# Two-layer metaformer: where the first sample's spectral rows, the filters and the inverse matrices lie between two stages

## The chip, the cores and the metric

The kernel runs on one core of a Trainium2 chip. The core has five engines with queues of their own: TensorE (PE, with PEld for its weight loads), VectorE (DVE), ScalarE (ACT), GpSimd (POOL) and SyncE (SP). SP issues most transfers here; ACT and POOL can issue transfers too. The metric is device microseconds from the first to the last instruction and what lies around them, as the median of several runs.

## What is computed

The input is 16 images of 128 channels by 32 x 32 pixels. The reference, cut to its steps:

```python
# layer 0
x = x + linear_attention(_ln_c(x))          # group norm, q/k softmax, context, projection
t = _to_tokens(x)
t = t + _L0_ffn_ref(_ln_t(t), ...)          # spectral filters (16 filters, FFT convolution) and 3 taps
x = _from_tokens(t, x)
# layer 1
x = x + _L1_conv_ref(_ln_c(x), ...)         # two 3x3 convolutions with batch norm, relu
t = _to_tokens(x)
t = t + _L1_ffn_ref(_ln_t(t), ...)          # 64 experts, each takes its 8 best tokens of a sample
x = _from_tokens(t, x)
```

In the spectral part, `U_plus` and `U_minus` are convolutions of every channel with 16 filters, mixed by `M_phi_plus` and `M_phi_minus` (128 x 128 matrices for each filter). The kernel does this in the frequency domain: at each frequency the spectrum of the samples is multiplied by one 128 x 128 matrix made from the filters.

## The kernel before

There are four stages, one after the other on PE, with overlap at the seams.

**Attention and spectra.** Sixteen samples run through a software pipeline. Each leaves its tokens in DRAM (`xd`) and its spectrum in DRAM (`vd`). The mixed filter matrices are gathered in the tile `mst`, 16 KB in each partition (L216, L685, L687).

**Frequencies.** Sixteen chunks `c` of frequencies. For each, `generate` (L805) makes the matrices from `mst` and `ph`, and `collect` (L816, L818) copies them into a tile `g` of 64 KB in each partition; there are two places for `g`, one for even and one for odd chunks. `multiply` (L829) multiplies the spectra of all samples with them. Chunk c+1 is generated while chunk c is multiplied, so in the last chunk, c = 15, there is only `multiply`. Its results are copied by ACT (L894), combined on DVE (L858, L859) into `ys`, finished (L843 to L846, on POOL, in the last chunk on DVE) and written by SP to the DRAM tensor `yd` in two transfers of 512 KB for each chunk (L850).

**Convolutions and gates.** For each sample b: `load(b)` (L1004) brings its tokens `xt[b]` (512 KB, L1008) and its spectral rows `y` (1 MB in two parts, L1011: 896 KB of rows of chunks 0 to 13, 128 KB of rows of chunks 14 and 15). Two places for `y` alternate between even and odd samples. Then come the small butterflies on POOL and DVE (L1024 to L1054), the `inverse` transform on PE (L1108, with the matrices `wi`, 1 MB, loaded at L956), `add` (L1115), a layer norm, two convolutions in a fast form (L988), the second norm, gates and pooling. The order of this work on every engine and on SP is written out by `planned` from a table with due ranks and is then fixed: an engine works its list in that order even if a later item is ready. In that list DVE has the first butterflies of sample 2 (`odd_sd`, `odd_turn`: L1037 to L1043) ahead of `ab_image` of sample 0 (L1174). POOL's `pair` (L1178) follows `ab_image`, and PE's `conv a` follows `pair`.

Before the list starts, `keep(ps, "cv", 26)` puts 26 matmuls without use on PE (L164, each shown as two rows), which follow the last `multiply`. For sample 0 POOL issues the tokens and the first part of `y`; SP issues everything else. On SP the order is `load(0)`, `load(1)`, then the convolution weights `cw` (two transfers of 1152 KB, L1477), four small biases (L1480, L1482), then `load(2)` and so on.

**Experts.** 32 weight halves of 1 MB go through a ring of 14 places, among them those of `y`, `wi` and `yo`; at the end the results are gated, added and written.

Places in SBUF: tiles of a later stage lie where those of an earlier one lay, and a transfer into such a place waits for the earlier tile's last reader. Adding up the tile sizes, `wi` before lies inside `mst`, whose last reader is the last `generate`.

Of the kernel before, what the change touches and what calls it, by code (L numbers as in the profile page):

```python
# [14 lines left out]
P = 128  # L15
# [15 lines left out]
NQ = 8  # L31
# [38 lines left out]
def metaformer_kernel(ctx: ExitStack, tc: tile.TileContext, io: dict, out: bass.AP):  # L70
# [2 lines left out]
    outs = out.rearrange("b c h w -> b c (h w)")  # L73

    const = ctx.enter_context(tc.tile_pool(name="const", bufs=1))


    ident = const.tile([P, P], F32, name="ident")
# [97 lines left out]
    with ExitStack() as l0:  # L176
# [36 lines left out]
            nc.vector.tensor_tensor(seg[:, i : i + 1], seg[:, i - 1 : i], hard[:, i : i + 1], ALU.add)  # L213
        coef = lconst.tile([P, NF], F32, name="coef")
        nc.vector.tensor_scalar(coef, wmix, sig, None, ALU.mult)
        mst = lconst.tile([P, EPR, C], F32, name="mst")  # L216
        ph = lconst.tile([P, NCH, CW], F32, name="ph")


        with ExitStack() as a0:  # L220
# [427 lines left out]
            def filters():  # L648

                wfm = setup.tile([P, NQ // 2, 2 * P], F32, name="wfm", tag="mi")  # L650
                nc.vector.tensor_scalar(wfm, wf[:, 1::2, :], -1.0, None, ALU.mult)

                def values(q, dst):
                    for sgn in range(2):
                        w = wfm[:, q // 2, :] if sgn and q % 2 else wf[:, q, :]
                        nc.tensor.matmul(
                            dst, phi[:, q, sgn, :], w, start=(sgn == 0), stop=(sgn == 1)
                        )

                yield  # L660
                xf = spectrum_tile()
                for parity in range(2):
                    pe = class_values(parity, values)
                    t = class_copy(pe, 1)
                    ts = class_copy(pe, ROT) if parity else t
                    ab = class_sums(parity, pe, t)
                    class_differences(parity, ab, pe, ts)
                    yield
                    for part in range(2):
                        butterflies(ab, xf, parity, part)  # L670
                    if parity:
                        butterflies(ab, xf, 1, butterflies(ab, xf, 1, 2))
                    yield
                half = CW // 2
                e, o = (xf[:, :, i].rearrange("p c r m j -> p c (r m j)") for i in range(2))
                nc.vector.tensor_tensor(ph[:, :, :half], e, o, ALU.add)
                nc.vector.tensor_tensor(ph[:, :, half:], e, o, ALU.subtract)
                for m in range(EPR // MB):
                    es = slice(m * MB, (m + 1) * MB)
                    for i in range(NF):  # L680
                        mi = setup.tile([P, MB, C], F32, name="mi", tag="mi")
                        nc.sync.dma_start(mi, io["M_phi"][i, :, es, :])
                        yield
                        if i == 0:
                            nc.vector.tensor_scalar(mst[:, es, :], mi, coef[:, 0:1], None, ALU.mult)  # L685
                        else:
                            nc.vector.scalar_tensor_tensor(  # L687
                                mst[:, es, :], mi, coef[:, i : i + 1], mst[:, es, :], ALU.mult, ALU.add
                            )

            def prepare():
# [84 lines left out]
        with ExitStack() as g0:  # L776
# [22 lines left out]
            def generate(c, q):  # L799

                pg = [psg.tile([P, 4, CW], F32, name="pg", tag="p") for r in range(RG)]
                for i in range(4):
                    for r in range(RG):
                        rs = slice(r * KR, (r + 1) * KR)
                        nc.tensor.matmul(  # L805
                            pg[r][:, i], mst[rs, 4 * q + i, :], ph[rs, c, :], start=True, stop=True,
                        )
                return pg

# [28 lines left out]
            def finish(c, ys):  # L838

                eng = nc.gpsimd if c + 1 < NCH else nc.vector  # L840
                e = cpl.tile([P, JL // RG, 2, C], F32, name="ye", tag="ye", bufs=1)
                yv = ys[:, :, 0]
                eng.tensor_tensor(e, yv[:, :, :2], yv[:, :, 2:], ALU.add)  # L843
                eng.tensor_tensor(yv[:, :, 2:], yv[:, :, :2], yv[:, :, 2:], ALU.subtract)
                eng.tensor_tensor(yv[:, :, 0], e[:, :, 0], e[:, :, 1], ALU.add)
                eng.tensor_tensor(yv[:, :, 1], e[:, :, 0], e[:, :, 1], ALU.subtract)  # L846
                for kl in range(JL // RG):
                    last = c + 2 >= NCH
                    j0 = kl * RG + (c - NCH + 2 if last else c) * JL
                    nc.sync.dma_start(  # L850
                        yd[last][j0 : j0 + RG].rearrange("g r b x e -> (g r b) (x e)"),
                        ys[:, kl].rearrange("p x m e -> p (x m e)"),
                    )
# [9 lines left out]
            with tc.manual_schedule(engines=PINNED):  # L863
                begin(0)
                gs[0] = gpl[0].tile([P, CW, C], F32, name="g", tag="g")
                for q in range(NB):
                    collect(0, q, generate(0, q))
                waiting = None
                for c in range(NCH):
                    if c + 1 < NCH:  # L870
                        gs[c + 1] = gpl[(c + 1) % 2].tile([P, CW, C], F32, name="g", tag="g")

                    ys = cpl.tile([P, JL // RG, 2, NM, C], F32, name="ys", tag="ys")
                    for m in range(NM):
                        if c + 1 < NCH:
                            pg = [generate(c + 1, 2 * m + x) for x in range(2)]
                            collect(c + 1, 2 * m, pg[0])
                        if waiting:
                            combine(*waiting)
                        if c + 1 < NCH:  # L880
                            if m == 0:
                                begin(c + 1)
                            collect(c + 1, 2 * m + 1, pg[1])
                        py = psg.tile([P, 2, JL // RG, C], F32, name="py", tag="p")
                        fresh = set()
                        for x in range(2):
                            multiply(c, m, x, py, fresh)
                        if c + 1 < NCH or m == 0:
                            t = cpl.tile([P, 2, JL // RG, C], F32, name="yt", tag="yt", bufs=1)
                        if c + 1 < NCH:  # L890
                            nc.scalar.copy(t, py)
                            waiting = c, m, ys, (t[:, 0], t[:, 1])
                        else:
                            nc.scalar.copy(t[:, m % 2], py[:, 0])  # L894
                            waiting = c, m, ys, (t[:, m % 2], py[:, 1])
                combine(*waiting)


# [11 lines left out]
    with ExitStack() as c1:  # L910
# [14 lines left out]
        FIRST = ("wi", "v", "cw0", "cw1", "p1", "y")  # L925
        halves = {}

        def load_half(h):

# [2 lines left out]
            if g >= E // EG:  # L932
                pr = AWAY[0] + h - 2 * (E // EG)
                if pr in AWAY:
                    tag = RING[(pr - AWAY[0] + 18) % len(RING)]
                    pool = first if tag in FIRST else xpool if tag[:2] == "xp" else work
# [5 lines left out]
            pool = first if tag in FIRST else xpool if tag[:2] == "xp" else work  # L942
            w = pool.tile([P, EG * HID], F32, name=f"we{n}", tag=tag, bufs=RING.count(tag))
            if n == 0:
                nc.sync.dma_start(
# [6 lines left out]
                )  # L952
            halves[h] = w

        wi = first.tile([P, NQ, 2, P], F32, name="wi", tag="wi")
        nc.sync.dma_start(wi, wid)  # L956
        cw = [first.tile([P, 3, NK, C], F32, name=f"cw{n}", tag=f"cw{n}") for n in range(2)]
        gw = cconst.tile([P, E], F32, name="gw")
# [13 lines left out]
        p2 = first.tile([P, 3 * PS - 1 + H * WP], F32, name="p2", tag="p2")  # L972
        nc.gpsimd.memset(p2, 0.0)
        abss = work.tile([P, 4, HT], F32, name="abss", tag="abss", bufs=1)
        yos = work.tile([P, 2, 4, HT], F32, name="yo", tag="yo", bufs=1)

        def of(p, first, step, n=2):

# [20 lines left out]
        def tokens(t):  # L999
            return t.rearrange("p (j c) -> p j c", c=C)  # L1000

        yts, xp = {}, {}

        def load(b):  # L1004
            if b % 2 == 0:
                xp[b // 2] = xpool.tile([P, 2, N], F32, name=f"xp{b // 2}", tag=f"xp{b // 2}")
            xt[b] = xp[b // 2][:, b % 2]
            (nc.sync if b else nc.gpsimd).dma_start(xt[b], xd[b])  # L1008
            yts[b] = first.tile([P, 2, 2 * NM, C], F32, name="y", tag="y", bufs=2)
            for i, js in enumerate((slice(P - 2 * JL), slice(P - 2 * JL, P))):  # L1010
                (nc.gpsimd if b + i == 0 else nc.sync).dma_start(  # L1011
                    yts[b][js].rearrange("p r x e -> p r (x e)"),
                    yd[i][:, :, b].rearrange("j r x e -> j r (x e)"),
                )

# [457 lines left out]
        with tc.manual_schedule(engines=PINNED | {mybir.EngineType.SP}):  # L1473
# [317 lines left out]
```

## Time and profile before

| | |
|---|---|
| median of 4 runs | 1242.4 us (1241.91 to 1244.41) |
| the profiled execution | 1238.34 us, of which its span is 1236.6 us |
| granted TensorE clock, mean | 0.993 |
| PE, DVE, ACT, POOL busy | 94%, 76%, 59%, 49% of the span |
| last `multiply` matmul begins | 652.3 us from the span's start |
| first `inverse` matmul of sample 0 begins | 667.5 us |
| first convolution matmul begins | 688.0 us |

Times inside the execution are microseconds from the span's start. A line of a timeline has the start, the length, the engine, the line of the kernel, the operation, what it writes and reads, and in brackets how long the engine was idle before it and what ended that. "SPq" is SP's queue issuing a transfer. In the chain of waits a row for DMA lasts from a transfer's issue to its landing. In the table of stretches the columns are the busy time of PE, PEld, DVE, ACT and POOL with the number of instructions, the granted clock, the busy share of the 16 DMA engines and what they moved in GB/s.

### The profile page before, as it was taken

The numbers are of one execution on the slowest core, as the hardware profiler recorded it, in microseconds if no ns is written. First come the engines' busy times: TensorE is split into PE (matmuls) and PEld (weight loads), VectorE is DVE, ScalarE is ACT, GpSimd is POOL, SyncE is SP. The second block draws the span as 40 slices with busy tenths as digits, with TensorE's granted clock in tenths as the row PEclk, the third lists the DMA queues.
The fourth block names the chain that finished last, engine by engine and source line by source line (L and its number), as shares of the span: only waits on it lengthen the run. The fifth ranks groups of instructions, "written<-read, shape, count | busy, mean of one in ns | idle before, by whom it ended". The sixth has DMA issues, their size and how long they took to land.

```text
span 1236.6 us, 34361 instructions
## 1 busy us (share of the span) xinstructions
PE 1158.5 (94%) x14398; PEld 952.8 (77%) x14398; DVE 936.6 (76%) x1944; ACT 724.8 (59%) x1420; POOL 603.6 (49%) x800
## 2 busy tenths in 40 slices
PE   6889999999999999999997899999999999998996
PEld 5677777777767889888887788888888888886453
DVE  5888888888766677677674689898988989876235
ACT  4777787777655777777670444565555565554211
POOL 2435454655568688888793433343433333230003
PEclk9999999999999999999998999999999999999998
DMA  7005334253436344443348611223333321406899
GB/s 281 24 31 169 120 114 156 94 171 102 154 120 197 97 137 135 132 130 128 111 135 272 160 52 52 86 76 120 95 120 116 107 86 68 154 34 224 318 403 383
DMA packets 91243, 175.14 MB, mean 142 GB/s; under 512 B 5968, under 2 KB 42064, under 8 KB 90448
## 3 DMA queue, kind: packets, MB, share of 16 engines
q1 hardware_dynamic: 90448, 170.46, 41.2%
q0 software_dynamic: 640, 2.49, 0.6%
q8 instruction: 113, 1.85, 0.6%
q14 instruction: 42, 0.34, 0.1%
HBM read 110.28 MB, written 62.65 MB: 140 GB/s over the span
## 4 chain that ended last, share of the span: by engine, by line
PE 55%; DVE 22%; issue 11%; ACT 5%; DMA 4%; POOL 2%; SPq 0%; POOLq 0%; DVEq 0%; ACTq 0%
PE pg L805 10%; PE pcv L988 10%; PE py L829 10%; PE big L638 6%; DVE bst L135 4%; PE big L171 3%; PE big L152 3%; PE big L570 3%; PE big L450 2%; PE big L533 2%; PE big L432 2%; DVE abss L1231 1%; DVE xp L1253 1%; DVE xp L1115 1%; ACT tt L144 1%
## 5 line engine op out<-in xcount | busy, mean ns | idle before, releaser
L988 PE MATMUL pcv<-v,cw 128*128 128x256 f32 x1152 | 258.2, 380 | 2.2 <-POOL v L1178 2.2
L988 PEld LDWEIGHTS pcv<-v,cw 128*128 128x128 f32 x1152 | 215.0, 190 | 35.0 <-issue 4.9
L818 ACT COPY g<-pg 128x512 f32<-128x512 f32 x316 | 161.1, 606 | 45.2 <-PE pg L805 44.5
L816 DVE COPY g<-pg 128x512 f32<-128x512 f32 x196 | 127.8, 683 | 72.1 <-PE pg L805 72.1
L805 PE MATMUL pg<-ph,mst 32*128 32x128 f32 x4096 | 142.7, 279 | 9.2 <-issue 7.9
L805 PEld LDWEIGHTS pg<-ph,mst 32*128 32x128 f32 x4096 | 127.6, 186 | 25.4 <-issue 15.9
L829 PE MATMUL py<-g,v 128*32 128x128 f32 x4096 | 124.9, 274 | 1.9 <-POOL v L797 1.2
L829 PEld LDWEIGHTS py<-g,v 128*32 128x32 f32 x4096 | 108.1, 110 | 9.8 <-POOL v L797 1.5
L144 ACT ACTIVATE tok<-tok,sts 128x128 f32<-128x128 f32 x256 | 101.9, 480 | 17.0 <-DVE sts L1065 13.6
L135 DVE BATCH_NORM_STATS2 bst<-big 128x6 f32<-128x256 f32 x256 | 91.2, 418 | 20.8 <-PE big L152 11.7
L796 POOL TENSOR_TENSOR v<-xc 128x256 f32<-128x256 f32 x128 | 99.6, 802 | 3.5 <-DMA xc<-vd 3.5
L638 PE MATMUL big<-u,mu 128*128 128x128 f32 (+4 forms) x384 | 86.1, 380 | 0.0
L1178 POOL TENSOR_TENSOR v<-abss 128x256 f32<-128x256 f32 x64 | 49.1, 787 | 68.1 <-DVE abss L1174 56.7
L286 POOL TENSOR_TENSOR xf<-ab 128x256 f32<-128x256 f32 x34 | 24.7, 727 | 110.6 <-DVE ab L253 110.6
L1197 POOL TENSOR_TENSOR yo<-abss 128x256 f32<-128x256 f32 x32 | 23.5, 734 | 108.6 <-DVE abss L1193 108.6
L638 PEld LDWEIGHTS big<-u,mu 128*128 128x128 f32 x384 | 56.8, 191 | 18.0 <-issue 15.3
L570 PE MATMUL big<-wf,ub 128*128 128x256 f32 x256 | 62.0, 385 | 0.2
L144 ACT ACTIVATE tt<-tt,sts 128x128 f32<-128x128 f32 x128 | 51.1, 480 | 14.6 <-DVE sts L1065 14.6
L797 POOL TENSOR_SCALAR v<-v 128x256 f32<-128x256 f32 x64 | 55.4, 866 | 5.6
L475 POOL TENSOR_TENSOR ke<-ke,ks 128x1024 f32<-128x1024 f32 x16 | 30.6, 1912 | 55.1 <-DVE qs L483 43.5
L570 PEld LDWEIGHTS big<-wf,ub 128*128 128x128 f32 x256 | 46.2, 190 | 8.7 <-ACT xn L423 3.0
L144 ACT ACTIVATE ub<-ub,sts 128x128 f32<-128x128 f32 x128 | 50.8, 481 | 0.0
(256 smaller groups left out, 2475.4 us busy)
## 6 DMA issues: line engine op xcount, KB each, us to landing
we<-in_weight SPq DMA_DIRECT2D x32, 1024.0 KB, 9.5
xc<-vd SPq DMA_DIRECT2D x64, 256.0 KB, 3.3
yd<-ys SPq DMA_DIRECT2D x32, 512.0 KB, 3.8
vd<-xf SPq DMA_DIRECT2D x15, 1024.0 KB, 5.1
y<-yd SPq DMA_DIRECT2D x15, 896.0 KB, 6.3
x<-in_x SPq DMA_DIRECT2D x16, 512.0 KB, 5.1
mi<-in_M_phi SPq DMA_DIRECT2D x16, 512.0 KB, 4.8
xd<-x SPq DMA_DIRECT2D x16, 512.0 KB, 6.3
```

Source lines behind the costliest of these rows:

```text
L135: nc.vector.bn_stats(bst[:, j : j + 2, :].rearrange("p j s -> p (j s)"), src[:, j : j + 2, :].rearrange("p j c -> p c j"),)
L144: nc.scalar.activation(dst[:, j, :], src[:, j, :], AF.Identity, bias=nm[:, j : j + 1], scale=r[:, j : j + 1],)
L570: nc.tensor.matmul(dst, self.ub[:, q, :], wf[:, q, :], start=True, stop=True)
L638: nc.tensor.matmul(self.pa[:, a:hi], mu[:, NF - 1 - si, tap, :], self.u[:, a - tap : hi - tap], start=(tap == 0), stop=(tap == KU - 1),)
L796: nc.gpsimd.tensor_tensor(vv[:, x, 1:, bs], e, o, op)
L797: nc.gpsimd.tensor_scalar(v[:, :, 0, bs], v[:, :, 2, bs], -1.0, None, ALU.mult)
L805: nc.tensor.matmul(pg[r][:, i], mst[rs, 4 * q + i, :], ph[rs, c, :], start=True, stop=True,)
L816: nc.vector.tensor_copy(dst, src)
L818: nc.scalar.copy(dst, src)
L829: nc.tensor.matmul(py[rows, x, kl, :], v[:, (x * NM + m) * JL + jl, 1 - ri : 3 - ri, :] .rearrange("p k b -> p (k b)"), g[:, ((x * 2 + ri) ...
L988: nc.tensor.matmul(pc[:, i], wt[:, dy, k, :], v[:, k, dy * WT : dy * WT + HT], start=(dy == 0), stop=(dy == 2),)
L1178: nc.gpsimd.tensor_tensor(v[:, k, WT : WT + HT], self.ab[:, 0], self.ab[:, 1], op)
```

## The change

The filters `mst` become two tiles of 8 KB that share a new pool, and a tag, with `y`; that pool lies ahead of all others and stays through the later stages. `y` of sample 0 therefore lies where the first half of `mst` lay, and `y` of sample 1 where the second half lay. `yo` goes from the pool `work` to `first`, `wi` from `first` to `work`, as the first tile there; by the sizes, it starts 6.5 KB into the 64 KB place of the odd chunks' `g`, which the last chunk uses.

The rows of sample 0 no longer come by `load(0)`. After the last chunk's matmuls have been put in the list, ACT issues two transfers from `yd`: the rows of chunks 0 to 13 and those of chunk 14. The last chunk's rows go from `ys` straight into `y` by four transfers of four partitions by 4 KB, two on SP and two on ACT, ahead of the writes to `yd`, which stay. The tokens of sample 0 come by SP instead of POOL, and for sample 1 `y` is issued ahead of the tokens. `keep` has 13 instead of 26.

```diff
+    ypool = ctx.enter_context(tc.tile_pool(name="ypool", bufs=2, reuse_waits="tile"))
+    yts = {}
+
+    def load_y(b, q, parts):
+
+        if b not in yts:
+            yts[b] = ypool.tile([P, 2, 2 * NM, C], F32, name="y", tag="y", bufs=2)
+        for j0, j1, i, k in parts:
+            q.dma_start(
+                yts[b][j0:j1].rearrange("p r x e -> p r (x e)"),
+                yd[i][k : k + j1 - j0, :, b].rearrange("j r x e -> j r (x e)"),
+            )
...
-        mst = lconst.tile([P, EPR, C], F32, name="mst")
+        mst = [
+            ypool.tile([P, EPR // 2, C], F32, name=f"mst{i}", tag="y", bufs=2) for i in range(2)
+        ]
+
+        def mrow(i, n=1):
+            h, k = divmod(i, EPR // 2)
+            return mst[h][:, k : k + n]
...
-                            pg[r][:, i], mst[rs, 4 * q + i, :], ph[rs, c, :], start=True, stop=True,
+                            pg[r][:, i], mrow(4 * q + i)[rs, 0], ph[rs, c, :], start=True, stop=True,
...
                 eng.tensor_tensor(yv[:, :, 1], e[:, :, 0], e[:, :, 1], ALU.subtract)
+                for kl in range(JL // RG if c + 1 == NCH else 0):
+                    for r in range(2):
+                        j0 = P - JL + kl * RG
+                        (nc.scalar if kl else nc.sync).dma_start(
+                            yts[0][j0 : j0 + RG, r].rearrange("p x e -> p (x e)"),
+                            ys[r * B :: 2 * B, kl].rearrange("p x m e -> p (x m e)"),
+                        )
...
+                load_y(0, nc.scalar, ((0, P - 2 * JL, 0, 0), (P - 2 * JL, P - JL, 1, 0)))
                 combine(*waiting)
...
-        wi = first.tile([P, NQ, 2, P], F32, name="wi", tag="wi")
+        wi = work.tile([P, NQ, 2, P], F32, name="wi", tag="wi", bufs=1)
         nc.sync.dma_start(wi, wid)
...
-        yos = work.tile([P, 2, 4, HT], F32, name="yo", tag="yo", bufs=1)
+        yos = first.tile([P, 2, 4, HT], F32, name="yo", tag="yo")
...
-            (nc.sync if b else nc.gpsimd).dma_start(xt[b], xd[b])
-            yts[b] = first.tile([P, 2, 2 * NM, C], F32, name="y", tag="y", bufs=2)
-            for i, js in enumerate((slice(P - 2 * JL), slice(P - 2 * JL, P))):
-                (nc.gpsimd if b + i == 0 else nc.sync).dma_start(
-                    yts[b][js].rearrange("p r x e -> p r (x e)"),
-                    yd[i][:, :, b].rearrange("j r x e -> j r (x e)"),
-                )
+            if b != 1:
+                nc.sync.dma_start(xt[b], xd[b])
+            if b:
+                load_y(b, nc.sync, ((0, P - 2 * JL, 0, 0), (P - 2 * JL, P, 1, 0)))
+            if b == 1:
+                nc.sync.dma_start(xt[b], xd[b])
...
-            keep(ps, "cv", 26)
+            keep(ps, "cv", 13)
```

The helper `pool_of` gives each tag of the expert ring its pool after the moves; the order of the ring is the same.

More of the change, by code (lines that the diff above doesn't have):

```diff
@@ L684, in filters @@
                         if i == 0:
-                            nc.vector.tensor_scalar(mst[:, es, :], mi, coef[:, 0:1], None, ALU.mult)
+                            nc.vector.tensor_scalar(mrow(m * MB, MB), mi, coef[:, 0:1], None, ALU.mult)
                         else:
                             nc.vector.scalar_tensor_tensor(
-                                mst[:, es, :], mi, coef[:, i : i + 1], mst[:, es, :], ALU.mult, ALU.add
+                                mrow(m * MB, MB), mi, coef[:, i : i + 1], mrow(m * MB, MB), ALU.mult, ALU.add
                             )
@@ L924, in metaformer_kernel, with pool_of @@
         )
-        FIRST = ("wi", "v", "cw0", "cw1", "p1", "y")
+        FIRST = ("yo", "v", "cw0", "cw1", "p1")
         halves = {}
+        def pool_of(tag):
+            return first if tag in FIRST else xpool if tag[:2] == "xp" else ypool if tag == "y" else work
         def load_half(h):
@@ L935, in load_half @@
                     tag = RING[(pr - AWAY[0] + 18) % len(RING)]
-                    pool = first if tag in FIRST else xpool if tag[:2] == "xp" else work
+                    pool = pool_of(tag)
                     x = pool.tile([P, 2, N], F32, name=f"xb{pr}", tag=tag, bufs=RING.count(tag))
@@ L941, in load_half @@
                 return
-            pool = first if tag in FIRST else xpool if tag[:2] == "xp" else work
+            pool = pool_of(tag)
             w = pool.tile([P, EG * HID], F32, name=f"we{n}", tag=tag, bufs=RING.count(tag))
@@ L1000, in tokens @@
             return t.rearrange("p (j c) -> p j c", c=C)
-        yts, xp = {}, {}
+        xp = {}
         def load(b):
```

## The prediction

> **What bounds the kernel now.** The page says PE, at 94% of the span, so a change at the seam of two stages is worth the PE idle time that it takes out there. I therefore read the chain of waits around the seam first: start, length, what.
>
> ```profile
> 645.22 7.41 PE py L829 x256
> ...
> 655.65 0.35 DVE ys L846
> ...
> 656.37 7.60 DMA yd<-ys
> ...
> 664.17 0.63 SPq L1011
> ...
> 677.09 11.29 DMA y<-yd
> ...
> 691.50 0.61 DVE abss L1174
> ...
> 692.18 0.73 POOL v L1178
> ...
> 692.95 5.45 PE pcv L988 x24
> ```
>
> The chain leaves PE with the last multiply at 652.63 and returns for good at 692.95, with conv a of sample 0. Between them are two round trips through DRAM: chunk 15's writes and the last part of sample 0's y (667.3), and then the queue of transfers that brings sample 2's y at 688.38. The timeline shows how the two hold the engines.
>
> ```profile
> 645.49 0.43 SPq L956 DMA_DIRECT2D wi<-wid  x1
> 652.55 11.49 PE L164 MATMUL wm<-ident 128*128 128x256 f32 x52
> 667.50 1.13 PE L1108 MATMUL big<-wi,y 128*128 128x128 f32 x8 [3.46 <-DMA y<-yd]
> 673.95 0.33 SPq L1008 DMA_DIRECT2D xp<-xd  x1
> 688.48 0.42 DVE L1037 TENSOR_TENSOR z<-y 128x256 f32<-128x256 f32 x1 [4.63 <-DMA y<-yd]
> 692.95 5.45 PE L988 MATMUL pcv<-v,cw 128*128 128x256 f32 x24 [2.17 <-POOL v L1178]
> ```
>
> The reader is to see that sample 0's y costs PE a late start (667.5), but that the second wait, sample 2's butterflies in front of `ab_image` in DVE's fixed list, decides when conv a starts. ACT had `image_copy` (L1165) done at 687.96, so `ab_image` could have run then; it ran at 691.50, and PE stood 2.17 us. Last the table of stretches, for the transfers:
>
> ```profile
> 654.00:656.00 2.00, 2.00 (x11) 1.77 (x10) 1.91 (x4) 0.00 (x0) 0.00 (x0) 1.00 0.94 217
> 656.00:658.00 2.00, 2.00 (x11) 1.77 (x10) 0.00 (x0) 0.00 (x0) 0.00 (x0) 1.00 0.97 373
> 658.00:660.00 2.00, 2.00 (x11) 1.74 (x11) 0.00 (x0) 0.00 (x0) 0.00 (x0) 1.00 1.00 404
> 662.00:664.00 2.00, 2.00 (x10) 1.46 (x8) 0.00 (x0) 0.00 (x0) 0.00 (x0) 1.00 0.12 47
> 672.00:674.00 2.00, 2.00 (x12) 2.00 (x11) 0.42 (x2) 0.00 (x0) 0.00 (x0) 0.50 0.89 228
> ```
>
> The DMA engines are full from 651.3 to 690 but for about 3.0 us (662.3 to 665.3), when SP waits for the writes to land.
>
> **The change, part by part.**
>
> *Direct rows.* They take out the write (656.0 to 663.97), SP's issue at 664.17 and its 3.1 us. In place: four transfers of 16 KB, issued at 656.0 to 656.9 when DVE is done. The nearest rows are the small loads `gb` and `tmat` (0.2 and 64 KB), 2.1 to 2.4 us to landing, so 658.2 to 659.3 if nothing is ahead of them in the queues. [...]
>
> *wi.* It goes from 645.49, an empty queue, to the last reader of chunk 15's `g`: not before 652.63. Alone it took 5.7 us, which gives 658.4. But chunk 14's writes (1.05 MB, from 651.3) are ahead of it on SP, and ACT's two loads of y (1.05 MB, issued from 653.1, after its last copy) run beside it: 3.15 MB. At 0.38 MB/us this is through at 659.6, and landed at about 660.4. I take 0.38 from the rows 373, 404 and 399 GB/s of 656 to 662, when loads and writes ran on two queues; in the 217 row the software queue was alone, and the change uses it no more. At 0.26 (the 652 to 654 row) it is 663.4. So inverse 0 starts at 660.4, 7.1 us earlier, with bounds 658.5 and 663.5.
>
> *Dummies.* 52 rows in 11.49 us, 0.221 each; 26 rows end at 658.3. The gap to the inverse is 2.1 us, against 3.46 now, after which the clock stood at 0.50 from 669 to 675 and the last 16 inverse matmuls took 3.79 us instead of the 2.05 of sample 1. [...]
>
> *Sample 0's chain.* DVE has sample 1's butterflies ahead of `stats` of sample 0 (677.88 now). Sample 1's second y part must still wait for chunk 15's writes; behind them and x0 it lands at about 669.8, two DVE pairs take 1.5 us, and `stats` begins at 671.5: 6.4 us earlier. So much is this chain worth if nothing else holds it; a warm clock doesn't change that.
>
> *Moved issues.* x0 goes to SP, behind chunk 15's writes; it lands by 664.5 and `add` needs it at 666.5 at the earliest, so it hides behind the inverse (6 us); without that cover it costs up to 1.4 us. ACT's four issues, 0.6 us each, and its wait for chunk 14's writes (2.6 us for such a write in a free queue, so about 654.5) cost nothing: after its last copy ACT is idle for 26.3 us. If they come late, only the two direct transfers behind them do. SP has two issues more (about 0.4 each) ahead of chunk 15's writes. A ninth transfer waits until that eight places before it has landed: x2 was issued at 673.95 when y1's first part landed (665.47 + 8.5). So chunk 15's second write probably waits for wi, to about 660; the queue is full until then, so nothing is added. POOL loses two issues of 0.7 us, off the path. Splitting `mst` and moving `yo` issue the same instructions into places as free as before; with no cover they would cost 0, bounds -0.5 and +0.5 us.
>
> *The queue up to sample 2's y.* What must pass first: chunk 14's writes, wi, y0, chunk 15's writes (1.05 MB each) and x0 (0.52): 4.72 MB from 651.3. At 0.38 this ends at 663.7. Then comes the list that began before at 667.3 (y0's last part landed) and ended at 688.38, 21.1 us: x1, y1, cw, biases, x2, y2. So y2 lands at 684.8. The first part at the 0.322 that 651.3 to 662.3 averaged before (3.54 MB in 11 us) gives 687.1; at 0.40, 684.2.
>
> *Sum.* From y2's landing to conv a it was 692.95 - 688.38 = 4.57 us. Conv a starts at the later of 690.78 - 6.4 = 684.4 (sample 0's chain without PE's 2.17) and 684.8 + 4.57 = 689.4: 3.6 us earlier. PE is 96% busy from 700 to 772 and 95 to 100% in every stretch of 24 us from there to 1110, and the later loads of y aren't awaited by it, so the 3.6 us pass to the end. The profiled 1238.34 becomes 1234.7; it lies 4.1 below the median shown, so I state 1242.4 - 3.6 = **1238.8 us**, own range 1237.7 to 1241.6 from the two rates and the 0.5 of the moved tiles.
>
> **Rivals.**
>
> *A. Sample 2's y doesn't bind.* If the list of 21.1 us runs as fast as its best rows (433 and 406 GB/s at 674 to 678), its 5.7 MB and the 0.7 that overtook it take 16 us, y2 lands at 679.7, and the chain of sample 0 decides: 6.4 us, 1236.0. For it: two queues run less with y alone. Against: loads of y took 6.1 to 6.4 us for 0.92 MB even in an empty queue.
>
> *B. The seam is DMA-bound and wi's megabyte eats the gain.* From 651.3 to y2's landing 10.1 MB moved in 37.1 us less 3.0 idle: 0.296 MB/us. With wi 11.1 MB at that rate take 37.6 us: y2 at 688.9, time 1242.9, no change. For it: the mean is the safest rate. Against: it contains the software queue's slow rows.
>
> *C. Slower: the same megabyte at the rate of the rows 668 to 674* (295, 244, 228, mean 0.256; y loads fill them, and there are more of these beside wi now). With a rate of 0.27 over the whole, y2 lands at 692.4 and the time is 1246.4. It decides by over 0.2% once the mean falls under 0.281 (11.1 MB by 690.8). Against: it would need to be below what before reached.
>
> **How the numbers follow.** Forecast 0.47, A 0.22, B 0.18, C 0.13. The measurement can tell 0.2%, 2.5 us, from no change: faster is below 1239.9. Of the forecast 0.38 lies there, 0.09 within; with A, faster is 0.60; same, with B, 0.27; slower 0.13. The range goes from 1235.0 (A with a shorter list) to 1243.5 (B with run spread), leaving out most of C.
>
> **What would show it.** Right: the first L1108 near 660.4, wi issued right after the last L829, y2's landing near 685 with DVE's L1037 still ended by DMA, conv a near 689. Wrong: L1037 not waiting (A); y2 at 688 or later though L1108 is early (B, C). If SP has wi behind chunk 15's writes, the inverse starts at 663 and the sum stays. If L1108 stays near 667, the direct rows aren't the last to land and my first step fails.

## The result and the profile after

The kernel became slower by a quarter of a per cent: 1245.56 us as the median of 53 runs (1238.27 to 1253.9), beside 1242.34 us for 77 runs of the kernel before; the ratio is 1.0024 with a 95% interval of 1.0013 to 1.0034, so between 1.6 and 4.2 us, and 3.0 in the middle. The forecast of 1238.8 was on the wrong side of it, and its range too low. The profiled execution took 1242.1 us (span 1240.3).

In the new profile the last `multiply` ends at 648.72 instead of 652.62, though nothing ahead of it runs other instructions. The frequency stage simply varies: over the sixteen profiles of this study it took from 266 to 279 us, with a mean of 274 us for both layouts (five and eleven profiles; with this spread a difference of 2 us between the layouts would not show). So all times of the seam are given below from the end of the last `multiply` in the same profile, written +10 for 10 us behind it. The mark for the whole seam is the first matmul of sample 2's `inverse`, behind conv a: from there to the last sample's `inverse` every kernel takes the same 354.3 to 354.9 us.

The chain of waits of the kernel after, in the same stretch as shown of before (start, length, what):

```profile
641.53 7.23 PE py L848 x256
...
651.77 0.35 DVE ys L865
...
652.13 0.66 SPq L869
...
653.93 6.82 DMA yd<-ys
...
660.83 0.60 SPq L84
...
671.77 11.05 DMA y<-yd
...
685.94 0.61 DVE abss L1203
...
686.62 0.73 POOL v L1207
...
687.39 7.08 PE pcv L1018 x24
```

It is the same chain as before; SP's two issues of direct rows (652.13 to 653.39) now stand in it, ahead of the writes. PE's own wait is still for sample 2's y. That y is in use at +34.2 (682.92 less 648.72), where it was at +35.9. And the end of the chain has a new row: conv a's 24 rows take 7.08 us, where they took 5.45. The timelines of the kernel after, by engine:

```profile
648.65 5.88 PE L176 MATMUL wm<-ident 128*128 128x256 f32 x26
648.81 0.32 SPq L986 DMA_DIRECT2D wi<-wid  x1
658.52 0.76 PE L1137 MATMUL big<-wi,y 128*128 128x128 f32 x2 [4.00 <-DMA y<-ys]
660.50 1.62 PE L1137 MATMUL big<-wi,y 128*128 128x128 f32 x6 [1.21 <-DMA y<-ys]
682.92 0.42 DVE L1066 TENSOR_TENSOR z<-y 128x256 f32<-128x256 f32 x1 [5.21 <-DMA y<-yd]
687.39 7.08 PE L1018 MATMUL pcv<-v,cw 128*128 128x256 f32 x24 [2.75 <-POOL v L1207]
```

Sample 0's rows are complete at +11.8, before at +14.7. The gain is 2.9 us, and it does not reach conv a: PE's gap in front of it grew from 2.17 to 2.75 us. The stretches say why conv a itself became longer (columns as before: busy PE, PEld, DVE, ACT, POOL, then granted clock, DMA share, GB/s):

```profile
656.00:658.00 2.00, 0.00 (x0) 0.00 (x0) 0.00 (x0) 0.00 (x0) 0.00 (x0) 0.65 1.02 363
658.00:660.00 2.00, 0.76 (x2) 0.50 (x2) 0.00 (x0) 0.00 (x0) 0.00 (x0) 0.50 0.98 358
666.00:668.00 2.00, 2.00 (x12) 2.00 (x10) 0.00 (x0) 0.00 (x0) 0.00 (x0) 0.50 0.96 305
686.00:688.00 2.00, 0.61 (x2) 0.52 (x3) 2.00 (x6) 0.09 (x1) 1.91 (x3) 0.83 0.97 221
688.00:690.00 2.00, 2.00 (x6) 1.64 (x5) 1.83 (x8) 0.42 (x2) 0.28 (x2) 0.50 0.40 137
```

After the 13 dummies PE stands from 654.5 to 658.5, the clock falls to 0.50 and is still there in the stretch 670 to 672. It falls a second time between 686 and 688 (a mean of 0.83, then 0.50), at the end of the gap in front of conv a; before, conv a ran at 1.00 (in the stretches from 692 to 700). The DMA engines are full until 688 (a share of 0.90 or more in every stretch of 2 us from 648). Together sample 2's `inverse` starts at +48.64, before at +48.67: the whole change moved nothing in the seam. So the 3 us lie behind the seam, or in the scatter ahead of it.

### The profile page after: what moved, and what is told of

The parts are those of the page before. It is cut to its first block, busy times and chain, and to the rows that moved or that the text cites. A ratio compares the mean times of both kernels' runs of the same rounds, so it can differ in the third digit from the quotient of the medians.

```text
span 1240.3 us, 34315 instructions
## 1 busy us (share of the span) xinstructions
PE 1159.5 (93%) x14372; PEld 953.5 (77%) x14372; DVE 938.4 (76%) x1944; ACT 724.9 (58%) x1420; POOL 601.8 (49%) x798
## 3 DMA queue, kind: packets, MB, share of 16 engines
q8 instruction: 113, 1.85, 0.6%
## 4 chain that ended last, share of the span: by engine, by line
PE 54%; DVE 22%; issue 11%; ACT 6%; DMA 4%; POOL 2%; SPq 1%; POOLq 0%; ACTq 0%; DVEq 0%
PE pg L824 10%; PE pcv L1018 10%; PE py L848 10%; PE big L657 6%; DVE bst L147 4%; PE big L164 3%; PE big L183 3%; PE big L589 2%; PE big L469 2%; PE big L552 2%; PE big L451 2%; DVE abss L1260 1%; DVE xp L1282 1%; DVE xp L1144 1%; ACT ub L568 1%
## 5 line engine op out<-in xcount | busy, mean ns | idle before, releaser
L824 PEld LDWEIGHTS pg<-ph,mst 32*128 32x128 f32 x4096 | 127.6, 186 | 21.9 <-issue 13.6
L156 ACT ACTIVATE tok<-tok,sts 128x128 f32<-128x128 f32 x256 | 101.9, 480 | 17.0 <-DVE sts L1094 13.6
```

Of the source, the lines that this page charges most:

```text
L156: nc.scalar.activation(dst[:, j, :], src[:, j, :], AF.Identity, bias=nm[:, j : j + 1], scale=r[:, j : j + 1],)
L824: nc.tensor.matmul(pg[r][:, i], mrow(4 * q + i)[rs, 0], ph[rs, c, :], start=True, stop=True,)
```

## The experiments

The table has all kernels that were run. "y2 in use" is DVE's first butterfly of sample 2, "gap" PE's idle time in front of conv a, "conv a" its 24 rows (a dash where conv a followed without a gap on conv c, the 12 rows of a convolution ahead of it), "inverse 2" the mark of the seam, "end" the time from the first gate matmul (L1624 in before) to the end. Ratios are to the kernel before, run beside it in the same batch; its medians there were 1244.91 (first four), 1245.37 (next four) and 1243.13 (next four). The last two have one run each.

| kernel | inverse 0 | y2 in use | gap | conv a | inverse 2 | end | ratio [95%] |
|---|---|---|---|---|---|---|---|
| before | +14.9 | +35.9 | 2.17 | 5.45 | +48.67 | 26.0 | |
| after | +9.8 | +34.2 | 2.75 | 7.08 | +48.64 | 27.2 | 1.0024 [1.0013, 1.0034] |
| after, 26 dummies | +11.3 | +35.1 | 4.69 | 7.13 | +49.62 | 26.1 | 1.0011 [0.9989, 1.0033] |
| after, `wi` early | +8.4 | +34.1 | 5.69 | 7.70 | +49.12 | 27.7 | 1.0046 [1.0025, 1.0066] |
| after, `wi` early, 26 | +11.3 | +33.4 | 5.27 | 7.12 | +47.86 | 26.3 | 1.0009 [0.9990, 1.0028] |
| before, 13 dummies | +10.9 | +33.3 | 4.96 | 7.89 | +48.56 | 27.6 | 1.0037 [1.0019, 1.0054] |
| after, 26, filters late | +12.1 | +30.3 | - | - | +44.86 | 26.2 | 0.9947 [0.9929, 0.9966] |
| before, filters late | +13.8 | +29.8 | - | - | +44.88 | 26.0 | 0.9976 [0.9955, 0.9997] |
| after, 26, order | +11.3 | +36.1 | - | - | +48.20 | 26.2 | 0.9986 [0.9969, 1.0004] |
| before, order | +14.8 | +38.7 | - | - | +49.42 | 26.0 | 0.9964 [0.9943, 0.9986] |
| after, 26, filters late, `wi` early | +11.3 | +28.2 | 0.26 | 5.45 | +41.06 | 26.3 | 0.9942 [0.9920, 0.9964] |
| the same with 13 | +7.9 | +29.8 | 1.25 | 5.45 | +42.65 | 27.9 | 0.9963 [0.9942, 0.9985] |
| before, 39 dummies | +16.9 | +33.5 | 1.85 | 5.45 | +46.31 | 26.0 | 0.9997 [0.9977, 1.0016] |
| after, 26, filters late, no direct rows | +22.0 | +36.8 | - | - | +51.85 | 26.4 | 1.0034 [1.0012, 1.0057] |
| after, 13 more at logits | +12.0 | +35.6 | 4.91 | 7.03 | +49.99 | 26.2 | one run |
| after, filters late, `wi` early, 13 more at logits | +7.7 | +28.4 | 0.88 | 5.45 | +41.17 | 26.4 | one run |

The scatter of the frequency stage is in every median, so a ratio alone can't tell two kernels of this table apart by less than about 0.2%; the columns of the seam can. Seam and ratio do not always agree: the two kernels with filters late and no other column far apart (+44.86 and +44.88, 26.2 and 26.0) have ratios 0.29% apart.

### First round: dummies or the queue

The two theories were called CLOCK (the 13 missing dummies let PE's clock fall) and QUEUE (the megabyte of `wi` and the order of transfers set the seam). Four kernels cross them.

Kernel after with 26 dummies:

```diff
-            keep(ps, "cv", 13)
+            keep(ps, "cv", 26)
```

> The changed kernel with 26 dummy matmuls again. Theory CLOCK (the 13 missing dummies let PE's clock fall to half at the seam, 657 to 673 and again from 687): the clock stays at 1.00 until the inverse, conv a of sample 0 runs its 24 rows in about 5.4 us instead of 7.1, the stretch from the last multiply to sample 2's first inverse matmul falls from 48.6 to about 47 us, and the median falls by 2 to 4 us below the changed kernel's, to the kernel before or up to 1.5 us under it. Theory QUEUE (wi's megabyte and the order of transfers set the seam, the clock is a side effect): the stretch stays within 0.5 us of 48.6 and the median stays about 3 us above before.

Measured: 1.0011, interval 0.9989 to 1.0033. Sample 2's `inverse` did not move forward; conv a in the profile is as slow as with 13, behind a longer gap, with a mean clock of 0.84 over 694 to 698 and 0.73 over 698 to 702:

```profile
688.96 2.76 PE L1018 MATMUL pcv<-v,cw 128*128 128x256 f32 x12
696.40 7.13 PE L1018 MATMUL pcv<-v,cw 128*128 128x256 f32 x24 [4.69 <-POOL v L1207]
```

So the dummies keep the clock in front of `inverse` 0 (1.00 from 664 to 680 us, that is +7 to +23, where the kernel after had 0.50 from about +8), and it is lost 30 us later: what sample 0's chain is earlier, PE waits longer for POOL's `pair`, and conv a pays for the wait a second time (7.13 us instead of 5.45 in before).

Kernel after with `wi` back in its early place (13 dummies), and the same with 26:

```diff
-        FIRST = ("yo", "v", "cw0", "cw1", "p1")
+        FIRST = ("wi", "v", "cw0", "cw1", "p1")
-        wi = work.tile([P, NQ, 2, P], F32, name="wi", tag="wi", bufs=1)
+        wi = first.tile([P, NQ, 2, P], F32, name="wi", tag="wi")
-        yos = first.tile([P, 2, 4, HT], F32, name="yo", tag="yo")
+        yos = work.tile([P, 2, 4, HT], F32, name="yo", tag="yo", bufs=1)
```

> The changed kernel with wi and yo back in their pools, so that wi lies under the even chunks' g, which is free before the last chunk's matmuls, and is loaded ahead of chunk 14's writes; 13 dummies as in the change. QUEUE: wi's 1.05 MB (about 2.8 us at 0.38 MB/us) leaves the seam's transfers, the direct rows land about 2.5 us earlier (9.3 us instead of 11.8 after the last multiply), sample 2's y 2.5 to 3 us earlier (31 to 31.6 us after it instead of 34.1), median about 2 to 3 us under the changed kernel. CLOCK: conv a still runs at half speed, the stretch to sample 2's inverse falls by under 1 us, median within 1 us of the changed kernel.

> wi early and 26 dummies. CLOCK and QUEUE each give their part: if both hold the stretch from the last multiply to sample 2's inverse falls to about 44.5 us (1.6 from the clock, 2.5 from the queue) and the median lies 3 to 5 us under the kernel before. If only CLOCK holds it is as with 26 dummies alone; if only QUEUE holds, as with wi early alone. If neither, it stays near 48.6 and the loss lies outside the seam.

Measured 1.0046 and 1.0009. Sample 0's rows came at +8.4 with 13, but sample 2's y was in use at +34.1 and +33.4, where it had been at +34.2 and +35.1 with the late `wi`: a gain of nothing and of 1.7 us, where 2.5 to 3 were expected, and with one and the same queue y2 scatters by 2.6 us (last section). QUEUE failed there.

The kernel before with 13 dummies:

> The kernel before with 13 dummies, nothing else. CLOCK: PE idles for 9 us instead of 3.5 ahead of sample 0's inverse, the clock falls earlier and the median rises by 1 to 4 us, about as much as the change did. QUEUE: PE waits there for transfers in any case, the median stays within 1 us of before.

Measured 1.0037. Of both pairs (13 against 26 with `wi` early; before with 13 against before) the one with 13 is slower by about 4 us in the medians, and by 2.8 to 3.0 us in the profiles from the last `multiply` to the end of the span. That looked like CLOCK, but for two things in the table: the seam accounts for +1.3 and -0.1 us of it, and the end column, 26.0 in the kernel before, is longer by 1.2 to 1.9 in every kernel with only 13, some 550 us behind the dummies.

### Second round: what decides conv a

If y2, which DVE's fixed list has ahead of `ab_image` of sample 0, decides conv a, then either bringing y2 sooner or taking it out of the way must move the seam. Filters late:

```diff
-            for n in range(2):
-                nc.sync.dma_start(cw[n], cwd[n])
+            nc.sync.dma_start(cw[0], cwd[0])
...
                     if b > 1:
                         load(b)
+                    if b == 2:
+                        nc.sync.dma_start(cw[1], cwd[1])
```

(The four bias transfers move with `cw[1]`.) On the kernel after with 26 dummies, and on the kernel before:

> After with 26 dummies; the second half of the filters (1.05 MB) and the four biases are issued behind y2 instead of in front of it, so y2 comes 4 to 5 us earlier than in the run with 26 dummies alone (last multiply to y2 in use +35.1 there). ORDER (sample 2's y, in front of ab_image of sample 0 on VectorE, is what decides): the 4.7 us of PE's gap in front of conv a go, conv a follows conv c at once and keeps the clock (24 rows 5.4 instead of 7.1 us), inverse 2 starts 4 to 4.5 us earlier than +49.6, time about 1241 beside 1245.3 for 26 dummies alone. CLOCK alone (what the seam needs is a warm clock): inverse 2 within 1 us of +49, time 1244 to 1246.

> Before with the same move of filters and biases behind y2. ORDER: y2 ceases to decide, sample 0's own late chain (inverse 0 at +14.9) does; conv a at about +38.1 instead of +40.3, inverse 2 at about +46.5 instead of +48.7, ratio about 0.998. Beside the run on after with 26 dummies the difference, about 2 us, is what the early rows are worth once y2 is out of the way. CLOCK alone: within 0.1% of before.

Measured 0.9947 and 0.9976; conv a follows conv c without a gap in both. The surprise is the seam: +44.86 and +44.88. With y2 out of the way the direct rows should have been worth 2 us, and they are worth nothing. The chain of waits of each tells why; first the kernel after with 26 and late filters:

```profile
656.86 8.40 DMA wi<-wid
665.28 4.75 DMA y<-ys
...
674.27 3.80 PE big L1137 x16
```

and the kernel before with late filters, whose last `multiply` ended at 661.42:

```profile
665.16 6.39 DMA yd<-ys
...
671.75 3.24 DMA y<-yd
...
679.20 3.51 PE big L1108 x16
```

In the first, the last of the direct rows come in at 670.03, that is +13.2 (656.79 subtracted). A DMA row of the chain begins with the issue, so the fourth direct transfer was issued only at 665.28, when `wi` had landed; `wi` waits for the end of the last `multiply` (it is issued 0.07 us behind it) and takes 8.40 us here. The other three were issued by 661.4. In the kernel after, the same wait would be short: it is read from the length of ACT's two issues, which take 2.21 us there and 1.14 us where `wi` is early:

```profile
652.24 2.21 ACTq L869 DMA_DIRECT2D y<-ys  x2
```

The first two `inverse` matmuls, which need two of the other three transfers, ran at 668.92 and the next at 670.16, so by estimate this wait accounts for 1.2 us; the rest is the slower passage beside `wi`, 6.8 and 7.1 us from issue to landing for SP's two direct transfers, which took 4.1 and 4.4 us with early `wi` and late filters (third round). In the second kernel, the round trip through DRAM ends at 674.99, that is +13.6. The edit exchanges one wait for another of the same length.

The order, changed by hand in the fixed list:

```diff
+        late = [(2, n) for n in ("even", "odd_sd", "odd_t", "odd_turn")]
+        order = [o for o in order if o not in late]
+        at = order.index((0, "pair")) + 1
+        order[at:at] = late
```

> After with 26 dummies; in the order that is written out by hand the four steps of sample 2's y (even, odd_sd, odd_t, odd_turn) come behind the pair of sample 0, so y2 lands as before but nobody in front of conv a waits for it. ORDER: gap in front of conv a gone, conv a directly behind conv c, inverse 2 at about +45 instead of +49.6, time about 1241; inverse 2's own wait for sample 2's y must then not take it back. CLOCK alone: inverse 2 within 1 us of +49.6.

> Before with the same four steps moved behind the pair of sample 0. ORDER: conv a about 2.2 us earlier, inverse 2 at about +46.5 instead of +48.7, ratio about 0.998; the difference to the run on after with 26 dummies, about 2 us, is what the early rows are worth. CLOCK alone: within 0.1% of before, inverse 2 within 1 us of +48.7.

The gap in front of conv a went in both, but the seam hardly got shorter: +48.20 where it was +49.62, and +49.42 where it was +48.67; +45 and +46.5 were expected. In the kernel after with the new order, ACT and PE now wait behind conv a:

```profile
700.40 0.88 ACT L156 ACTIVATE tok<-tok,sts 128x128 f32<-128x128 f32 x2 [5.44 <-DVE sts L1094]
```

DVE does sample 2's butterflies where it used to do the norm of sample 1, and `terms` of sample 1 waits for that norm. The fixed list has only one place for this late work, and what stands behind it waited: 5.44 us on ACT here. The second kernel's ratio of 0.9964 isn't explained by its seam; its later stages in the profile are those of before, and it stays open. Either something in it was not seen, or a median of twelve runs can be off by more than its interval says.

### Third round: what `wi` costs and what the direct rows bring

With the filters late, y2 no longer hides the rest. Early `wi`, 26 dummies and late filters on the kernel after (the diffs above together), and the same with 13:

> After with 26 dummies, the filters' second half and the biases behind y2, and the inverse matrices back in their early place (loaded about 5 us before the last multiply ends), so nothing large stands in the queue ahead of sample 0's y. QUEUE (the megabyte of inverse matrices, issued at the last multiply's end, takes 8.4 us on the way of y0 and eats what the direct rows save): y0 lands at about +8.5 instead of +13.2 (late matrices) and +13.7 (rows through memory, early matrices), and inverse 2 starts at +40 to +41 instead of +44.9; time 3 to 5 us under the run with late matrices (1239.1). Rival (the chain behind y0, or y1 and y2, sets the seam once y0 is near +13): inverse 2 stays within 1 us of +44.9.

> The same with 13 dummies. CLOCK: the clock falls before inverse 0, whose rows and those of the next inverses run at half speed; inverse 2 1 to 2 us later than with 26, the end 1.2 us longer, ratio to the run with 26 about 1.002 to 1.003. QUEUE alone: dummies to +3 do not stand in front of inverse 0, which starts up to 3 us earlier (+8.4 instead of +11.3), and the two are equal or 13 is the faster.

Measured 0.9942 (1237.42 us, the fastest median of the study; 7 runs) and 0.9963. The seam came as expected, but the time is only 1.7 us under that of the kernel with the late `wi`, not 3 to 5, and by the ratios (0.9942 and 0.9947) the two are equal within their intervals. The timeline of PE in the first:

```profile
653.10 11.49 PE L176 MATMUL wm<-ident 128*128 128x256 f32 x52
664.43 1.05 PE L1137 MATMUL big<-wi,y 128*128 128x128 f32 x8
682.89 2.75 PE L1018 MATMUL pcv<-v,cw 128*128 128x256 f32 x12
685.90 5.45 PE L1018 MATMUL pcv<-v,cw 128*128 128x256 f32 x24 [0.26 <-POOL v L1207]
```

`inverse` 0 follows the dummies without a wait, at a clock of 1.00 (660 to 672), and sample 2's `inverse` starts at +41.06: 3.8 us sooner than with the late `wi` (+44.86), and 3.8 us sooner than without direct rows (+44.88). So the late place of `wi` costs 3.8 us of the seam, and the direct rows, together with the issues that moved with them (the second comparison changes both), are worth the same 3.8 us where nothing large is ahead of them. QUEUE was right after all for sample 0's rows; y2 came 2.1 us sooner, which is within its scatter.

The late `wi` without direct rows, that is, the same kernel as "after, 26, filters late" with the last 32 rows of sample 0 through DRAM again:

```diff
-                for kl in range(JL // RG if c + 1 == NCH else 0):
...
                 combine(*waiting)
+                load_y(0, nc.gpsimd, ((P - JL, P, 1, JL),))
```

> After with 26 dummies and the filters late, but the last 32 rows of sample 0 go through memory again, loaded on GpSimd's queue: the late place of the inverse matrices alone. QUEUE: the writes of the last chunk wait behind the megabyte as the direct rows do, y0 lands 3 to 5 us later than with direct rows (+16 to +18 instead of +13.2), inverse 2 at about +48 instead of +44.9, ratio to the run with direct rows about 1.003. Rival (the direct rows are worth nothing because the matrices themselves come last): y0 and inverse 2 within 1 us of +13.2 and +44.9.

Measured 1.0034, and sample 2's `inverse` at +51.85, 7.0 us behind the kernel with direct rows. PE's idle time ahead of the first `inverse` matmul:

```profile
678.28 2.05 PE L1131 MATMUL big<-wi,y 128*128 128x128 f32 x8 [10.53 <-DMA xp<-xd]
```

(The profile names the tokens; in the same timelines DVE ends a wait for y at 678.10.) The direction was as QUEUE said, the size more than twice as large: the write, whose landing ends POOL's wait at 669.79, and the reading back follow one another behind `wi`. But the reading back also changed its queue: POOL's took 8.3 us from 669.79, where SP's took 3.24 us in the kernel before with late filters. So the 7.0 us are not the price of the late `wi` alone; against this way of loading, the direct rows are needed to break even.

The kernel before with 39 dummies:

> Before with 39 dummies instead of 26; they end near +9, y0 is there at +14.7, so they stand in nobody's way. CLOCK as a matter of the seam: the gap in front of inverse 0 becomes about 6 us at most as before or shorter, matmuls of inverse 0 run at full clock, inverse 2 0 to 0.5 us earlier, within 0.1% of before. If the end of the kernel (26.0 us with 26 dummies, 27.2 to 27.7 with 13) goes with the number of dummies it stays at 26.0.

Measured 0.9997, the end at 26.0. I had counted rows as dummies: a dummy is shown as two rows, so the 39 end at about +17, and `inverse` 0 waits for them to +16.9, two us later than before. Nothing else is late for that: sample 2's `inverse` is at +46.31. Sample 0's chain in the kernel before had room, since y2 decides.

### Fourth round: the end

Open was why 13 dummies in the seam lengthen the end. The last transfer of instructions (queue q8, one packet of 0.02 MB) had been found 23 to 25 us before the end with 26 dummies, 27 with 39, and 20 to 21 with 13. Two kernels with 13 in the seam got 13 more far behind it:

```diff
-        idle = {(13, "turn"): 4, (13, "pooled"): 8, (15, "logits"): 11, (15, "turn"): 1}
+        idle = {(13, "turn"): 4, (13, "pooled"): 8, (15, "logits"): 24, (15, "turn"): 1}
```

> After with its 13 dummies, and 13 more at a place late in the kernel where TensorE waits 0.6 us (logits of the last sample: 24 instead of 11), so that TensorE's instruction stream is as long as with 26 in the seam, but the seam is after's. CODE (the last transfer of instructions, 0.02 MB on one DMA engine, which lies 21 us before the end with 13 dummies, while the results are written, and 24 to 28 us before the end with 26 and 39, lets one DMA engine finish 1.2 us late): from the gates to the end 26.0 to 26.4 us as with 26, not 27.2 to 27.9. If it is the dummies of the seam themselves: 27.2 or more. The 13 added cost up to 2.5 us between the last inverse and the experts either way.

> The kernel with early inverse matrices, filters late and 13 dummies, and the same 13 more at the logits of the last sample. CODE: from the gates to the end 26.0 to 26.4 us instead of 27.9, and the last transfer of instructions 24 us or more before the end. If it is the dummies of the seam: 27.5 or more.

Measured: the end is 26.2 and 26.4 us, where it was 27.2 and 27.9, with the seam's 13 unchanged. (The 13 more cost 4.1 to 4.8 us where they stand, more than the 2.5 allowed for.) The transfer of instructions as the view of the DMA queues has it, over one us, in the kernel after (1219.3 to 1220.3):

```profile
q8 instruction: 1, 0.02, 8.2%
```

and the issues of results on SP in the same kernel:

```profile
1216.42 4.37 SPq L1664 DMA_DIRECT2D out<-xp  x4
1220.88 11.18 SPq L1664 DMA_DIRECT2D out<-xb  x10
```

It falls into the writing of the results, 3 us behind their first issue. In the kernel with 13 more at the logits it lies at 1226.8 to 1227.8, with the first result issued at 1227.92:

```profile
q8 instruction: 1, 0.02, 6.5%
```

In kernels with 13 the results' last 1.1 to 1.8 us move only 18 to 36 GB/s, about what one of sixteen engines would have of the 400 GB/s ahead of that (25 by estimate); with 26 or 39 the rate falls from 400 to nothing at once. My reading is that the 13 removed dummies shorten PE's instruction stream, that the last block of it is fetched when the results are being written, and that one engine finishes late. That these are PE's instructions is inferred from their place: in the kernel before, the packet starts 1.4 us ahead of the first gate matmul with 39 dummies, 2.7 us behind it with 26 and 6.9 us behind it with 13. That the place of this transfer goes with the longer end is shown by the two kernels; that it is this packet which holds the engine up is inferred.

## Why the prediction was wrong, by its steps

**The bound.** That sample 2's butterflies in front of `ab_image` decide conv a was right: with y2 five to six us earlier (4.8 and 6.1) the gap went, on both kernels.

**Direct rows and `wi`.** The first matmul with all of sample 0's rows was forecast for 660.4 and came at 660.50, but that agreement is chance: the last `multiply` ended 3.9 us sooner. Counted from it, the forecast was +7.8 and the measurement +11.8. The term that was mis-sized is the passage of the direct rows. They were put at 2.1 to 2.4 us and ahead of `wi`, which was to land last, at 660.4 (+7.8). In the kernel after, the fourth direct transfer was issued at 653.91; if it was held until `wi` had landed, as in the chain of the kernel with 26 and late filters (665.26 and 665.28), `wi` was there sooner than that, at about +5.2. The fourth transfer then kept PE waiting until 660.50, 6.6 us from its issue, and those issued at 652.13 and 652.24 until 658.52, 6.3 to 6.4 us. Beside them on the 16 engines were ACT's two loads of y and chunk 15's writes, with a stretch at 363 GB/s. The hold itself was foreseen ("a ninth transfer waits"), but for chunk 15's second write, where it would have added nothing. The gain at sample 0 was 2.9 us instead of 7.1.

**The queue up to y2.** The sum put 12.4 us on the 4.72 MB that pass first and 21.1 us on the list behind them, and so y2 3.6 us earlier; measured were 1.65 (landing +34.1 against +35.75). Even that is no gain of the change: the kernel before with 13 and with 39 dummies had y2 at +33.3 and +33.5 with its old queue. The mean over the three profiles of before's queue (before, with 13, with 39) is +34.2, over the three with after's queue (after, with 26, with 13 more at the logits) +35.0. Rival B (the megabyte of `wi` eats the gain, no change) is what the seam did; it had no term for the clock or the end. C was right in the sign, but its mechanism, a y2 later than before, did not come.

**The last step, from y2 to conv a and on.** The 4.57 us from y2's landing to conv a held exactly (682.82 to 687.39). But conv a was carried over at its old length, and there the step "the 3.6 us pass to the end" failed even for the 1.65 us that the profile has: conv a took 7.08 us instead of 5.45, 1.6 us more.

**Dummies.** The sum has no term for them, and this failed in two ways. The forecast gap of 2.1 us was 4.0, and the clock fell to 0.50 in it: a mean of 0.65 over 656 to 658, between 1.00 and 0.50, puts the fall at 656.6, which is 2.1 us behind the dummies' end at 654.5. Behind the 2.75 us gap in front of conv a the clock was 0.50 too (688 to 690). And fewer dummies lengthen the end of the kernel, by 1.2 us in this profile and 1.2 to 1.9 over all with 13, together with a later place of the last instruction transfer. The views on which the prediction rests don't show this.

**Sample 0's chain, moved issues, split tiles.** The chain was forecast 6.4 us earlier; its rows came 2.9 us earlier, and DVE's statistics (671.72 in the new profile) began at +23.0 instead of +25.3. As said, that cost or brought nothing by itself, since y2 decides. No row of the waits names the split `mst`, `yo` or sample 0's tokens.

**What the 3.0 us are made of.** The medians point at the dummies: the kernel before with only 13 is slower by as much as the whole change or more (1.0037, interval 1.0019 to 1.0054), while for the change with 26 no loss is shown (1.0011, interval 0.9989 to 1.0033). The profiles place only a part of it. The end has 1.2 to 1.9. The seam has 0.0 between the two first profiles; over three profiles each, the mark is at +49.4 for after's `wi` and filters (+48.64, +49.62, +49.99) and at +47.8 for before's (+48.67, +48.56, +46.31), which would be 1.6, about what conv a's longer rows cost in the profile of after (7.08 less 5.45). The sum, 2.8 to 3.5, lies in the interval of 1.6 to 4.2, but the seam's part rests on three profiles with a spread of 2.4, and in the kernel before with 13 the seam has no loss at all, so it is possible, not shown. Between the last sample's `inverse` and the experts the kernel after took 95.7 us and before 94.8; over the kernels without more dummies there it is 95.5 to 96.0 in all four with 13 and 94.8 to 95.9 in the ten others, and this too stays open. The profile of after has another 5.6 us between experts and gates (65.43 us against 59.85), with PE waiting 3.4 for expert weights; no other kernel with 13 dummies had more than 60.4 there, and I put it down to that one execution.

## What to carry to other kernels

A transfer that is moved out of a chain must be priced with what is queued ahead of it in its new place: on the seam the direct rows, with the issues that moved along, saved 3.8 us, and the megabyte that was displaced in the same change cost 3.8 us, in part because the issue of one direct transfer waited for its landing. Earlier work in front of a wait that stayed was not merely worth nothing here: PE stood longer at that wait (2.75 us in the kernel after and 4.69 with 26 dummies, where it was 2.17), and conv a's 24 rows behind it took 7.08 and 7.13 us instead of 5.45, at a clock of 0.50 over 688 to 690 in the first and a mean of 0.73 over 698 to 702 in the second. Look first for the transfer that may go behind the one that decides: moving a megabyte of filters behind y2 brought 3.8 us on the old kernel's seam, and together with early `wi` and the direct rows 7.6 us. By the ratios the time fell by 3.0 and 7.2 us.

## What had not been expected of the hardware

**The clock behind short gaps.** Over the kernels with a gap in front of conv a, its 24 rows took 5.45 us behind every gap of 0.26, 0.88, 1.25, 1.85 and 2.17 us, and 7.03 to 7.89 us behind every gap of 2.75, 4.69, 4.91, 4.96, 5.27 and 5.69 us. None of these gaps lies between 2.17 and 2.75 us. Among the longer ones the price (1.6 to 2.4 us) hardly goes with the gap. The clock behind the gap was 1.00 with 2.17 us (before, 692 to 700), 0.50 over 688 to 690 with 2.75 us (after), and a mean of 0.73 over 698 to 702 with 4.69 us (after with 26 dummies). These lengths belong to this place: in the kernel after with 26 and late filters the clock was 1.00 in every stretch of 2 us from 656 to 670, but its mean over 655 to 675 was 0.92 and over 675 to 690 0.88. With 0.50 while it was down, that puts the fall at about 671.7 by estimate, though PE's only gaps since the dummies had been 0.71 and 0.79 us, among `inverse` matmuls.

**The place of an instruction fetch.** Twenty-six matmul rows taken out of PE's stream at 650 us moved a fetch at 1215 us by some 4 us against the gates and the results behind them; with it came an end that is 1.2 to 1.9 us longer.

**Scatter of landings.** With the same queue of transfers y2 was in use between +33.3 and +35.9. A forecast of 3.6 us from one profile's landing is not far above that.
